# A recurrence beside a large product: sums written into PSUM ahead of the product, GpSimd's work moved, empty instructions spread

## The chip, the core and the metric

The kernel runs on one core of a Trainium2 chip. Five engines work side by side, each through its own list of instructions in order: TensorE (PE, with its weight loads shown as PEld), VectorE (DVE), ScalarE (ACT), GpSimd (POOL) and SyncE (SP), which here only starts DMA transfers. They wait for one another through semaphores. SBUF is the core's working memory, PSUM the memory that TensorE writes to, eight banks of 512 floats in each of 128 partitions. The metric is the time of the whole program on the device, in microseconds.

## The reference

All tensors are float32. With x of 64 x 256 x 1024 and a condition of 64 x 1024:

```python
xW = jnp.einsum('ntd,dh->nth', x, Wx) + b
def step(prev_h, xw):
    next_h = jnp.tanh(prev_h @ Wh + xw)      # 256 steps, one after the other
    return (next_h, next_h)
x = x + h_t                                   # layer 0: residual
# layer 1: a gate from the condition, on a Haar transform and its inverse
h = silu(cond @ W1.T + b1); gate = sigmoid(h @ W2.T + b2)
x = x + (v + a)    # a: v transformed, times gate, transformed back
```

The gate is the same for all coefficients of a channel, so the transform and its inverse cancel and the second layer is a factor (2 + gate) for each sequence and channel. What remains is a large product x @ Wx, a recurrence of 256 steps that each need h @ Wh, tanh and a residual, and a multiplication by the factor.

## The kernel before, in words

**Stages.** The first 12 steps (`ALONE`) and a stretch of plain products for the first 16 pairs of steps (`FIRST`) are set up code. The steady part runs from step 12 to 255 and takes about nine tenths of the time. Two steps make a pair; `xT[i]` is the input of pair i.

**The steps of h.** Each step is one h @ Wh by a scheme of seven products on quadrants (Strassen-Winograd). In the order of TensorE they are: m1 into `m16`, product 4 into `accs[2]`, product 2 into `accs[0]`, m5 into bank `main0`, m6 into `m16`, m7 into bank `main1`, product 3 into `accs[1]`. Between them ScalarE copies m1 to `y` (L989) and m6 to `u` (L1024), VectorE forms the four quadrants of h (L1010, L1027, L1028, L1032, L1035, L1038), ScalarE applies tanh (L971), VectorE transposes each quadrant (L975) and forms the sums for the next step (L244 to L247). `put_part` (L639) writes the next step's x @ Wx into the banks that accumulate.

**The products beside h.** x @ Wx is computed for later pairs by the same scheme on a larger scale, in the order of `ORDER`: units of two pairs, four units to a chunk (`U`), so 28 products of a chunk, numbered 0 to 27 here, four for each of the seven forms. One product (`Product.multiply`, L824) is 12 matmuls of 128x512 in fp32r: the float32 operands are split in high and low parts, four matmuls go into a bank `mixed`, eight into a bank `main`. Two steps of h and then 3 or 4 products make a group (`M`, `counts`, `beside_x`); a chunk of products is spread over eight groups as 3, 4, 3, 4 and so on. Weights of a form are 3 MB, loaded from DRAM by `load_weights` two forms ahead.

**Around a product.** `Form` prepares an operand three products ahead: VectorE masks the high bits (L795), forms x2 (L800) and x1 (L807), ScalarE casts x0 (L809); the form of p = 5 starts with a sum (L781). Afterwards `take_mixed` copies the bank `mixed` with ScalarE (L859) and GpSimd adds to it (L860) either a bias row or the state `u` of the unit; `finish` adds the bank `main` with VectorE (L868) and, for four forms, stores the result. `reload` brings it back in the layout of h. Other GpSimd work is put off to the first of the two steps (`pool_later`): differences of the quarters of x for p = 5 and 6 (L770), `u` plus or minus `v` after p = 6 and 7 (L876), and, as its first item, the scaling of a finished pair by the factor (L520, two instructions). The last product's `finish`, with the first half of a form (L795, L800), comes in the first step behind the copy of m1; its second half (L807, L809) behind the copy of m6 (`slot`).

**Order.** All engines of the steady part run in the order in which the program is written; none is planned by a scheduler.

**Alignment.** TensorE's instructions are fetched in blocks of 256 (`BLOCK`). `addr_align(BLOCK, PLACE)` fills up with empty instructions until the next one has place 60 in its block. It stands before the last two matmul positions of a group of 3 or 4, so that block edges fall at the same places of each group.

Of the kernel before, what the change touches and what calls it, by code (L numbers as in the profile page):

```python
# [61 lines left out]
P = 128  # L62
# [7 lines left out]
KB = B // 2  # L70
# [15 lines left out]
FORMS = 3  # L86
ORDER = (1, 2, 5, 6, 3, 7, 4)
BLOCK = 256
PLACE = 60
# [3 lines left out]
def tile_cond_resid(  # L93
# [425 lines left out]
    def scale(x, s: int) -> None:  # L519
        nc.gpsimd.tensor_mul(of_step(x, s), of_step(x, s), blocks(factor))  # L520
# [248 lines left out]
    def pool_sub(out, a, b) -> None:  # L769
        nc.gpsimd.tensor_sub(out, a, b)  # L770

    class Form:


        def __init__(self, n: int):
            self.n = n
            self.c, self.p, self.v = ups[n]
            a = {q: quarters.get((self.c, self.v, q)) for q in PLACES}
            if self.p == 5:
                self.src = forms.tile([P, HALF], F32, tag="s1", bufs=1, name=f"s1_{n}")  # L780
                nc.vector.tensor_add(self.src, a[21], a[22])  # L781
                self.later(lambda: (pool_sub(a[21], a[11], a[21]), pool_sub(a[11], a[22], a[21])))
            else:
                self.src = a[{1: 11, 2: 12, 6: 11, 3: 12, 7: 21, 4: 22}[self.p]]
            if self.p == 6:
                self.later(lambda: (pool_sub(a[12], a[12], a[11]), load_quarter(self.c + 1, self.v, 11)))
            made[n] = self
# [26 lines left out]
    class Product:  # L814
# [9 lines left out]
        def multiply(self, aligned: bool) -> None:  # L824
            f, w = made.pop(self.n), weights[self.m]

            def one(out, x, j: int, start: bool, stop: bool) -> None:
                for k in range(KB):
                    if aligned and j == 0 and k == KB - 2:
                        nc.tensor.addr_align(BLOCK, PLACE)  # L830
                    nc.tensor.matmul(  # L831
                        out=out,
                        lhsT=x[:, k * P : (k + 1) * P],
                        rhs=w[j][:, cols(k)],
                        start=start and k == 0,
                        stop=stop and k == KB - 1,
                    )

            one(self.mixed, f.x2, 2, True, True)
            one(self.main, f.x1, 1, True, False)  # L840
            one(self.main, f.x0, 0, False, True)
# [7 lines left out]

        def take_mixed(self) -> None:  # L850

            p = self.p
            if p in (1, 5):
                t = self.new_state("u" if p == 1 else "v")
                add = b_row[:, cols(0 if p == 1 else 1)]
            else:
                t = halves_x.tile([P, HALF], F32, tag="o", bufs=3, name=f"o_{self.n}")
                add = self.state("u")
            nc.scalar.activation(t, self.mixed, AF.Copy, scale=-1.0)  # L859
            nc.gpsimd.tensor_add(t, t, add)  # L860
            self.t = t
# [30 lines left out]
    slot = []  # L892

    def form(n: int, late: bool = False) -> None:

        f = Form(n)
        f.first()
        if late:
            slot.append(f.second)
        else:  # L900
            f.second()

    def prepare(late: bool = False) -> None:

        if formed[0] < min(len(ups), done[0] + FORMS):
            form(formed[0], late)
            formed[0] += 1

    def beside_x(t: int, n: int) -> None:

        before = None
        for j in range(n):
            m = done[0]
            u = Product(m, (n - 1 - j) % 2 ^ 1)
            u.multiply(n > 2 and j == n - 1)
            done[0] += 1
            if j == 0:
                residual(t, hT)
            if before and (before.c, before.v) == (u.c, u.v):
                before.finish()  # L920
                before = None
            u.take_mixed()
            if j == 0:
                accs[:] = [put_part(t + 1, o) for o in range(3)]
            if before:
                before.finish()
            before = u
            if last_of_product(m):
                load_weights(u.m + 2)
            if j + 1 < n:  # L930
                prepare()
        if n == 0:
            residual(t, hT)
            accs[:] = [put_part(t + 1, o) for o in range(3)]
        else:
            slot.append(lambda: (before.finish(), prepare(True)))
# [16 lines left out]
    counts = []  # L953
    for c, n in enumerate(UNITS):
        counts += [7 * n * (g + 1) // sizes[c] - 7 * n * g // sizes[c] for g in range(sizes[c])]
    groups = [M] * len(counts) + [2 * M]
    first = ALONE
    for t in range(ALONE, T):
# [30 lines left out]
        nc.scalar.copy(y[:, 0], m16)  # L989
        if slot:  # L990
            slot.pop(0)()
        if s == 0 and i > ALONE // S and i - 1 in pairs and i < NP - 1:
            scale(pairs[i - 1], 0)
            scale(pairs[i - 1], 1)
        if s == 0:
            for f in pool_later:
                f()
            pool_later.clear()
            if i + 1 < NP:
# [22 lines left out]
        put_next(0)  # L1022
        strassen_product(m16, sides[6], 6)
        nc.scalar.copy(u, m16)  # L1024
        if slot:
            slot.pop(0)()
# [76 lines left out]
```

## Time and profile before

| | us |
|---|---|
| time, median of 2 runs (3645.45 and 3645.54) | 3645.49 |
| the profiled execution's own time | 3618.79 |
| its span | 3616.7 |
| TensorE busy | 3092.5 |
| VectorE busy | 2654.7 |
| GpSimd busy | 1387.4 |
| ScalarE busy | 1050.9 |
| mean granted TensorE clock, share of full speed | 0.955 |

The profile is of one execution. Busy time is the time in which an engine has an instruction under way; a busy TensorE is not one at its peak, because matmuls overlap. The table of waits names for each wait the engine and line that waited, what ended the wait, the total, the number of times and the longest. "issue" means that nothing the profile shows ended it. The timeline lists instructions in order of time, with the idle time before them in brackets. A window is a stretch of the span with the busy time of each engine, the granted clock, and the share of time that the DMA engines were busy.

### The profile page before, as it was taken

The page shows a single profiled execution, that of the slowest core. Times are in us where ns is not written, and L with a number is a line of the kernel's source. Part 1 is how long each engine was busy: PE and PEld are TensorE (multiplying, and loading weights), DVE is VectorE, ACT ScalarE, POOL GpSimd, SP SyncE. Part 2 cuts the span into 40 slices and gives each one's busy share as a digit, 9 for nine tenths or more (in the row PEclk, how much of TensorE's full clock was granted, in tenths as well). Part 3 has the DMA queues.
Part 4 walks back from the last instruction along what each step waited for, and adds up shares of the span by engine and source line. Part 5 has one row for each costly group of instructions (what it writes and reads, how often), then busy time and mean ns, then how long its engine had stood idle before and what let it go on. Part 6 is the DMA issues. An engine that isn't in the chain of part 4 may idle for free.

```text
span 3616.7 us, 149916 instructions
## 1 busy us (share of the span) xinstructions
PE 3092.5 (86%) x63190; PEld 2674.6 (74%) x63190; DVE 2654.7 (73%) x6017; ACT 1050.9 (29%) x3097; POOL 1387.4 (38%) x985
## 2 busy tenths in 40 slices
PE   9976888888989888888888889888898888888788
PEld 6865777777777777777777777777777777777677
DVE  7553777877868677786777868678686777877665
ACT  3111223323323233332233323232232233322222
POOL 2241343543435344353443434335243343534231
PEclk9988999999999999999999999999999999999899
DMA  7555556565565656565465564655556565655565
GB/s 272 180 183 212 173 194 220 180 226 179 205 213 186 215 188 216 184 215 208 158 222 200 190 230 165 222 176 200 201 185 217 185 211 177 214 200 190 180 223 185
DMA packets 273087, 721.45 MB, mean 199 GB/s; under 512 B 56240, under 2 KB 122544, under 8 KB 232112
## 3 DMA queue, kind: packets, MB, share of 16 engines
q1 hardware_dynamic: 272288, 711.34, 56.6%
q8 instruction: 515, 8.44, 0.9%
q14 instruction: 140, 1.15, 0.1%
q10 hardware_dynamic: 144, 0.52, 0.0%
HBM read 553.39 MB, written 158.33 MB: 197 GB/s over the span
## 4 chain that ended last, share of the span: by engine, by line
PE 60%; DVE 14%; issue 14%; DMA 5%; POOL 3%; ACT 2%; SPq 1%; DVEq 0%; POOLq 0%; ACTq 0%
PE acc L214 15%; PE main L831 14%; PE m_h L214 10%; PE main_h L214 10%; PE mixed L831 7%; DMA w<-form 3%; DVE x L807 2%; PE main L293 2%; DVE high L795 2%; DVE y L1027 2%; POOL o L860 1%; ACT h L971 1%; DVE hT L975 1%; DVE h L1032 1%; PE m L214 1%
## 5 line engine op out<-in xcount | busy, mean ns | idle before, releaser
L831 PE MATMUL main<-w,x 128*128 128x512 f32 x3136 | 813.1, 396 | 167.6 <-issue 161.9
L831 PEld LDWEIGHTS main<-w,x 128*128 128x128 f32 x3136 | 580.0, 188 | 336.2 <-issue 205.5
L860 POOL TENSOR_TENSOR o<-o,u 128x512 f32<-128x512 f32 x280 | 388.1, 1386 | 959.6 <-ACT o L859 934.0
L971 ACT ACTIVATE h<-h 128x128 f32<-128x128 f32 x976 | 275.5, 306 | 842.8 <-DVE h L1010 611.5
L831 PE MATMUL mixed<-w,x 128*128 128x512 f32 x1568 | 434.6, 399 | 0.7 <-issue 0.7
L214 PE MATMUL m_h<-wh,hT 128*32 128x128 f32 x7808 | 299.2, 299 | 134.4 <-DVE s L247 47.4
L809 ACT CAST x<-high 128x512 fp32r<-128x512 f32 x392 | 243.8, 622 | 540.5 <-DVE high L795 480.7
L214 PEld LDWEIGHTS m_h<-wh,hT 128*32 128x32 f32 x7808 | 229.7, 119 | 204.6 <-issue 128.6
L214 PE MATMUL main_h<-t,s 128*32 128x128 f32 x7808 | 281.7, 277 | 90.1 <-issue 89.5
L214 PE MATMUL acc<-t,hT 128*32 128x128 f32 x8160 | 309.1, 296 | 53.7 <-DVE hT L975 45.5
L831 PEld LDWEIGHTS mixed<-w,x 128*128 128x128 f32 x1568 | 285.2, 188 | 77.9 <-issue 23.9
L795 DVE TENSOR_SCALAR high<-a 128x512 int32<-128x512 int32 x336 | 334.1, 994 | 11.8 <-DMA a<-xT 11.7
L800 DVE SCALAR_TENSOR_TENSOR x<-high,a 128x512 fp32r<-128x512 f32 x336 | 319.7, 951 | 29.0 <-DVE high L795 1.8
L975 DVE STREAM_TRANSPOSE hT<-h 128x128 f32<-128x128 f32 x972 | 298.0, 307 | 52.5 <-ACT h L971 52.3
L520 POOL TENSOR_TENSOR x<-x,factor 128x512 f32<-128x512 f32 x242 | 328.7, 1380 | 10.6 <-DVE x L644 5.7
L214 PEld LDWEIGHTS m_h<-t,s 128*32 128x32 f32 x7808 | 227.4, 114 | 125.1 <-issue 101.6
L214 PEld LDWEIGHTS acc<-t,hT 128*32 128x32 f32 x8160 | 258.4, 121 | 69.9 <-DVE hT L975 57.4
L214 PE MATMUL m_h<-t,s 128*32 128x128 f32 x7808 | 274.5, 282 | 17.2 <-ACT y L989 12.7
L214 PE MATMUL acc<-wh,hT 128*32 128x128 f32 x8160 | 284.8, 280 | 2.5 <-issue 2.5
L214 PE MATMUL acc<-wh,s 128*32 128x128 f32 x8160 | 279.7, 276 | 3.8 <-issue 3.8
L860 POOL TENSOR_TENSOR u<-u,b_row 128x512 f32<-128x512 f32 x56 | 87.0, 1553 | 507.1 <-ACT u L859 505.6
L214 PE MATMUL main_h<-wh,s 128*32 128x128 f32 x7808 | 274.9, 281 | 5.9 <-issue 5.9
(118 smaller groups left out, 4622.1 us busy)
## 6 DMA issues: line engine op xcount, KB each, us to landing
w<-form SPq DMA_DIRECT2D x315, 1024.0 KB, 8.2
x<-xT SPq DMA_DIRECT2D x137, 512.0 KB, 4.2
yT<-x SPq DMA_DIRECT2D x122, 512.0 KB, 10.6
a<-xT SPq DMA_DIRECT2D x224, 256.0 KB, 3.5
xw<-sum_b SPq DMA_DIRECT2D x896, 64.0 KB, 3.3
sum_b<-o SPq DMA_DIRECT2D x168, 256.0 KB, 3.3
sum_b<-u SPq DMA_DIRECT2D x56, 256.0 KB, 3.8
form<-wx SPq DMA_DIRECT2D x36, 256.0 KB, 5.7
```

The source lines that it names most:

```text
L214: nc.tensor.matmul(out=out[q * R : (q + 1) * R], lhsT=a[:, k * R : (k + 1) * R], rhs=wh_s.sides[i][k][:, q], start=first and k == 0, stop= ...
L293: nc.tensor.matmul(out=acc[h], lhsT=v[:, k * P : (k + 1) * P], rhs=wx_s[k][which][:, h * HALF : (h + 1) * HALF], start=start and k == 0, s ...
L520: nc.gpsimd.tensor_mul(of_step(x, s), of_step(x, s), blocks(factor))
L795: nc.vector.tensor_scalar(out=self.high, in0=self.src[:].bitcast(I32), scalar1=HIGH, scalar2=None, op0=ALU.bitwise_and)
L800: nc.vector.scalar_tensor_tensor(out=self.x2, in0=self.high, scalar=1.0 + DOWN, in1=self.src, op0=ALU.mult, op1=ALU.subtract)
L807: nc.vector.tensor_sub(self.x1, self.src, self.high)
L809: nc.scalar.copy(self.x0, self.high)
L831: nc.tensor.matmul(out=out, lhsT=x[:, k * P : (k + 1) * P], rhs=w[j][:, cols(k)], start=start and k == 0, stop=stop and k == KB - 1,)
L860: nc.gpsimd.tensor_add(t, t, add)
L971: nc.scalar.activation(quad(h, j), quad(h, j), AF.Tanh)
L975: nc.vector.transpose(quad(hT, j), quad(h, j))
L1027: nc.vector.tensor_add(y[:, 3], y[:, 3], u)
```

## The change

- A product's `mixed` bank no longer begins empty. `preload` has ScalarE write the negated bias row or state `u` into the bank before the product, whose first matmul no longer clears it; so the copy with scale -1 (`take_mixed`) yields the sum, and the GpSimd addition is gone. The first product of a group is written in the second step of h (`coming`), the others one product ahead.
- The list of GpSimd work in the first step is reordered, the differences and sums first and the scaling last, and its first instruction waits for ScalarE's copy of m1 (`behind`, `mark`).
- The last form of a group is prepared whole, and in the second step instead of in two halves in the first: `slot` is now emptied behind the copy of m1 alone, one entry a step.
- In `beside_x` the previous product's `finish` comes ahead of `take_mixed`, and the residual and `put_part` behind it.
- The alignment stands in every product of a group of 3 or 4, with places 39 (three) or 30 (four) apart that end at 70 (`SPREAD`, `PLACE`), and is given up after the first group of another size.
- `counts`: a group takes at least 3 products in full chunks, and rounding is upward: 4, 3, 4, 3 instead of 3, 4, 3, 4.

```diff
+SPREAD = {3: 15, 4: 6}
-PLACE = 60
+PLACE = 70
...
+    def behind(ins, other) -> None:
+        tc.add_manual_dep(
+            ins.ins,
+            other.ins.name,
+            mybir.DependencyInfo(mybir.DependencyClass.Sync, mybir.DependencyReason.DATA),
+            reason="GpSimd works beside the products of h",
+        )
...
-                    if aligned and j == 0 and k == KB - 2:
-                        nc.tensor.addr_align(BLOCK, PLACE)
+                    if place is not None and j == 0 and k == KB - 2:
+                        nc.tensor.addr_align(BLOCK, place % BLOCK)
...
-            one(self.mixed, f.x2, 2, True, True)
+            one(self.mixed, f.x2, 2, False, True)
...
+        def preload(self) -> None:
+            prior = {1: b_row[:, cols(0)], 5: b_row[:, cols(1)]}.get(self.p)
+            nc.scalar.activation(self.mixed, self.state("u") if prior is None else prior, AF.Copy, scale=-1.0)
+
         def take_mixed(self) -> None:
...
-            nc.scalar.activation(t, self.mixed, AF.Copy, scale=-1.0)
-            nc.gpsimd.tensor_add(t, t, add)
-            self.t = t
+            nc.scalar.activation(self.t, self.mixed, AF.Copy, scale=-1.0)
...
+    def coming(n: int) -> None:
+        if n:
+            products.append(Product(done[0], (n - 1) % 2 ^ 1))
+            products[0].preload()
+
     def beside_x(t: int, n: int) -> None:
         before = None
+        aligned[0] &= n in SPREAD
         for j in range(n):
             m = done[0]
-            u = Product(m, (n - 1 - j) % 2 ^ 1)
-            u.multiply(n > 2 and j == n - 1)
+            u = products.pop()
+            u.multiply(PLACE - (n - 1 - j) * (24 + SPREAD[n]) if aligned[0] else None)
             done[0] += 1
-            if j == 0:
-                residual(t, hT)
...
             if before:
                 before.finish()
             before = u
+            if j + 1 < n:
+                nxt = Product(m + 1, (n - 2 - j) % 2 ^ 1)
...
+                nxt.preload()
+                products.append(nxt)
+            if before:
+                u.take_mixed()
+            if j == 0:
+                residual(t, hT)
+                accs[:] = [put_part(t + 1, o) for o in range(3)]
...
-            slot.append(lambda: (before.finish(), prepare(True)))
+            slot.append(lambda: before.finish() if before else None)
+            slot.append(prepare)
...
-        counts += [7 * n * (g + 1) // sizes[c] - 7 * n * g // sizes[c] for g in range(sizes[c])]
+        for g in range(sizes[c]):
+            least = need + -(-7 * n * (g + 1) // sizes[c])
+            counts.append(min(len(ups), max(least, sum(counts) + 3 if n == U else 0)) - sum(counts))
+        need += 7 * n
...
-        nc.scalar.copy(y[:, 0], m16)
+        mark = nc.scalar.copy(y[:, 0], m16)
         if slot:
             slot.pop(0)()
-        if s == 0 and i > ALONE // S and i - 1 in pairs and i < NP - 1:
-            scale(pairs[i - 1], 0)
-            scale(pairs[i - 1], 1)
         if s == 0:
-            for f in pool_later:
-                f()
+            todo = list(pool_later)
             pool_later.clear()
+            if i > ALONE // S and i < NP - 1:
+                todo += [lambda r=r: scale(pairs[i - 1], r) for r in range(S)]
+            for k, do in enumerate(todo):
+                ins = do()
+                if k == 0:
+                    behind(ins, mark)
...
+        if last_of_group and not final:
+            coming(counts[0])
         strassen_product(m16, sides[6], 6)
         nc.scalar.copy(u, m16)
-        if slot:
-            slot.pop(0)()
```

## The prediction

> **What bounds the kernel now.** I read the page's head and chain first. TensorE (PE) is busy 86% of the span and holds 60% of the chain that ended last, but a seventh of that chain is "issue", time in which the engine waited for nothing that the profile names.
>
> ```profile
> span 3616.7 us, 149916 instructions
> PE 3092.5 (86%) x63190; PEld 2674.6 (74%) x63190; DVE 2654.7 (73%) x6017; ACT 1050.9 (29%) x3097; POOL 1387.4 (38%) x985
> PE 60%; DVE 14%; issue 14%; DMA 5%; POOL 3%; ACT 2%; SPq 1%; DVEq 0%; POOLq 0%; ACTq 0%
> ```
>
> GpSimd (POOL) is at 38%: its additions are off the chain, and taking them away gives nothing by itself. So I asked who PE waits for.
>
> ```profile
> PE main L831 <- issue: 161.9, 106, 7.6
> PE main_h L214 <- issue: 95.3, 48, 3.3
> PE m_h L214 <- DVE s L247: 47.4, 21, 2.5
> PE acc L214 <- DVE hT L975: 45.5, 41, 2.0
> ```
>
> The first row is the dearest wait, and it is the alignment's own. The trace holds runs of empty instructions on PE's sequencer, 110 runs beside x, 73.5 ns for each instruction: 50 to 52 (3.8 us) in a group of three products, 26 to 28 (1.9 us) in a group of four. Just behind them the last two matmuls of the group come 2.1 us late (three) or 0.35 us (four); PE's queue covers the first 1.65 us. A group's numbers close: 896 slots of two steps, 72 of three products, 4 to 6 waits and 50 to 52 empty ones make 1024.
>
> Then one period of eight groups by the table of windows, each from one start of products to the next (columns: time, busy us and instructions by engine, granted clock, DMA share, GB/s).
>
> ```profile
> 1943.56:1966.56 23.00, 21.02 (x488) 18.77 (x485) 17.65 (x47) 7.83 (x25) 6.82 (x5) 1.00 0.20 67
> 1966.56:1994.08 27.52, 24.13 (x501) 20.88 (x497) 24.67 (x53) 8.73 (x27) 14.57 (x10) 1.00 0.54 202
> 2044.97:2072.52 27.55, 23.13 (x489) 19.83 (x485) 18.27 (x47) 7.84 (x25) 9.96 (x7) 0.94 0.71 243
> 2072.52:2102.60 30.08, 25.87 (x501) 22.35 (x497) 21.78 (x51) 8.90 (x27) 9.62 (x7) 0.95 0.64 225
> ```
>
> The first is undisturbed but for its empty instructions: 8.5 us of products, 2.1 of gap, 12.3 of two h steps. The others have the same steps in 14 to 19 us. The timeline gives two reasons. **DMA:** in the last window,
>
> ```profile
> 2081.93 1.46 SPq L760 DMA_DIRECT2D w<-form  x3
> 2094.57 1.08 PE L214 MATMUL main_h<-t,s 128*32 128x128 f32 x31
> 2098.14 0.27 PE L214 MATMUL main_h<-t,s 128*32 128x128 f32 x1 [2.49 <-issue]
> ```
>
> 3 MB of weights are issued 2.2 us before the steps, and the DMA engines are full until about 2096. The 16 KB block with PE's next 256 instructions is asked for 256 instructions ahead (3.5 us in h): here its packet began 3.9 us after the block ahead was entered, and PE went on 2.3 us after that. In the quiet first window the packets begin 0.1 to 0.9 us after, and nothing stalls. **GpSimd against VectorE (DVE):**
>
> ```profile
> 1959.13 0.29 DVE L1027 TENSOR_TENSOR y<-y,u 128x128 f32<-128x128 f32 x1
> 1982.60 6.16 POOL L770 TENSOR_TENSOR a<-a,a 128x512 f32<-128x512 f32 x4
> 1986.21 1.35 DVE L1027 TENSOR_TENSOR y<-y,u 128x128 f32<-128x128 f32 x1
> ```
>
> A VectorE instruction that reads SBUF alone waits until the GpSimd instruction under way ends (0.29 becomes 1.35 us); those that read PSUM, and the transposes, keep their times.
>
> **The change part by part.** Durations are of the profiled execution (3618.8 us, of which 3616.7 are the span); the median of the timed runs is 3645.5, 0.7% longer, so I take differences from the profile and set them on the median.
>
> A. *Empty instructions spread.* By the orders of both programs they stay 4,350 (4,779), but no run is longer than 22 (1.62 us, at the first product of three; then 13 to 15 for each product; at most 10 with four). All lie under the 1.65 us that the queue covers, and 2.7 us apart it fills again. So the first row goes: -162 us. If it doesn't fill, the cost is what it was (bounds -162 to 0). Four-product groups give 0.35 us each of this, the five gaps over 7 us (behind groups of two) about 37 in all.
>
> B. *Clock.* The trace grants half the clock in 76 stretches, most of 3.41 us; 26 stand behind these gaps, each up to 1.7 us: -44 at most, 0 at least if another gap takes their place. I take -35, since most have no other gap near. By the Trainium skill ("TensorE: Matmul & The Clock Gate", What's actually happening) the clock falls only after an idle window of about 3.4 us; by that rule gaps of 2 us cost no clock and B is nothing. The trace disagrees: the window from 2044.97 shows 0.94 with no PE gap above 2.5 us.
>
> C. *Sums through PSUM.* 392 GpSimd additions (1.39 us) go and 392 ScalarE (ACT) writes into a bank come; nearest rows 0.59 us (PSUM to SBUF) and 0.58 (SBUF to PSUM, 128x512, L256), so 0.6. ScalarE then has 1.8 us of work for each product of 2.7: hidden. Its place: a group's first write stands in step two behind tanh of quadrant 0 and ahead of the copy of u; the next product's stands ahead of taking the present bank, ready over 1 us before its product. If ScalarE waited here, the copy of u and three tanh would. On its inputs it doesn't: u's GpSimd sum, where there is one, comes first in the list and ends by 2.9 us. Products lose waits on the main bank (rows of 4 to 12 us): counted at 0, bounds -12 and +13 (0.3 us in the third of groups whose step two ends late).
>
> D. *The last form moves from step one to step two.* In step one VectorE no longer runs L795 and L800 ahead of L1010, nor L807 ahead of L1027. In the second window (DVE late, no DMA stall) steps take 15.9 us instead of 12.3; I get 14.2 there, below. Thirteen such groups: -30 with what the others save (bounds -45, 0). In step two it costs 0.43+0.69+0.68 = 1.8 us between the residual (ends 2.7 us into the step) and L1010, which PE allows at 2.9: L1010 starts at 4.6, tanh and the first bank write end at 5.9, and products can start at 6.2. Hidden by 0.3 us, unless GpSimd is still at work.
>
> E. *GpSimd begun behind y's copy, sums of forms first, scales last.* It starts 1.5 us into step one, one instruction each 1.28 us when alone, and by turns with VectorE's SBUF instructions. Its list is 2 to 5 instructions long in six groups of eight (over by 8.2 us), 9 and 7 in two (forms 9 to 12; forms 13 to 15 with two sums of u). With 9: the turns put L1027 at 5.4 us, L244 to L247 at 8.2, 9.7, 11.2 and 12.7 (undisturbed 7.3 to 8.0), the residual at 14.2, the form at 14.9, L1010 at 16.7, tanh, bank write, and the products start at 18.0: 5.7 us over 12.3, before 1.8. With 7: 15.6, 3.3 over, before 1.5. Four, with a form that adds L781: products at 13.3 and up to 0.9 later in their bank waits. The two long lists cost 3.9+1.8 = 5.7 us a period, 13 periods: +74. Bounds 0 (a form's wait is hidden) and +110 (half clock behind the 4 us gap as well).
>
> F. *Groups are 4,3,4,3 instead of 3,4,3,4.* A weight load follows products 3, 7, 11 and so on of each 28. Before, the group of products 0 to 2 has none (23.00 us); now 0 to 3 ends with one, its DMA lying wholly over the two steps, as before only with product 27 (last window of the period, 29.23 us: steps 17.4). So +5 in that group; group 4 to 6 becomes free, but was without DMA stall already. The four others near h stay within 1 us of what they were: earlier by product, but without 2 us of gap as a head start. 13 periods at 5, less 5: +60 (bounds 0 and +90). The Trainium skill ("Runtime: NRT & Kernel Launch", Instruction fetch mechanics) has instruction fetch hidden by the slow issue; by it F is nothing. The 2.49 us row above speaks against it.
>
> PLACE 60 to 70 moves block edges by 10 slots, 0.14 us in h: nothing. The tail after the first group of two has no alignment; its edges fall anywhere, 11 groups, 0 +-10.
>
> Sum: -162-35-30+74+60 = -93. 3645.5-93 = **3552**.
>
> **Rivals.**
> 1. *The gain is kept*: E and F stay near 0, since the six short lists end before L244 and the loads find other gaps. For it: the second window's four subtractions cost before only through the form in step one, which is gone. Against it: the turns in the timeline. -162-35-30 = -227: 3418; half of it 3485.
> 2. *The change doesn't do what it says*: the queue doesn't fill between runs and the row of 161.9 stays. Against it, groups of four with 1.9 us of empty instructions lose only 0.35. Then -30+74+60: 3750; with E and F nothing, 3615.
> 3. *Slower*: the first product waits for the bank write, this for tanh, L1010 and a form that takes turns with GpSimd, in all groups and not in two of eight. It decides once GpSimd's work reaches 8 us into h everywhere, for instance with scales that wait. At the 3.3 us of the list of seven in 75 further groups: +248, 3800. Slower by over 2% from 2.2 us a group on. Against it: six lists end by 8.2 us.
> 4. *Clock by the skill's rule*: the gaps of 2 us cost no clock, so B is 0: 3587.
>
> **How the numbers follow.** Forecast 0.58 (3480 to 3640), rival 1 0.22, rival 2 0.08, rival 3 0.06, rival 4 0.06. A change of 2%, 73 us, is about what can be told from none here. Of the forecast six in ten lie below 3572.6: 0.35, with rival 1 0.57 faster. Slower by over 2%: half of rival 2 and all of 3, 0.10. The rest, 0.33, within. The range 3420 to 3670 leaves out the low end of rival 1 and the dear ends of 2 and 3.
>
> **What would show it.** A: the wait of the products' main bank on issue falls from 161.9 to below 30. B: 50 to 60 half-clock stretches for 76. C: no GpSimd line among the products, ScalarE's writes at 0.6 us. D: steps without long list or load near 12.3. E: one window in eight with steps near 18 and GpSimd busy over 12 us. F: the window of products 0 to 3 above 27 us with a stall on issue at main_h. The prediction is wrong if the products' first matmul waits for ScalarE in most groups, or if no steps take long beside a load.

## The result, and the profile after

The changed kernel took **3468.5 us** (median of 2 runs, 3466.1 and 3470.9), beside 3645.5 for the kernel before: a ratio of **0.9514, 95% interval 0.9474 to 0.9555**. The forecast was 3552 us with a range of 3420 to 3670, so the sign and the range held, but the gain is 177 us where the forecast had 93. It lies between rival 1 (3418) and its half (3485). The runs below show that the terms of the sum were wrong by more than their sum.

The page of the profiled execution (3466.1 us, mean granted clock 0.966 for 0.955), its head and its chain:

```profile
span 3464.3 us, 148882 instructions
...
PE 3061.6 (88%) x63190; PEld 2678.8 (77%) x63190; DVE 2348.7 (68%) x6017; ACT 1269.8 (37%) x3489; POOL 792.0 (23%) x593
...
q8 instruction: 513, 8.40, 1.0%
...
PE 74%; issue 10%; DVE 6%; DMA 5%; POOL 2%; ACT 2%; SPq 1%; DVEq 0%; POOLq 0%; ACTq 0%
```

PE now holds 74% of the chain (60%), VectorE 6% (14%). GpSimd lost 595 us of busy time, far more than the span lost. The waits of PE (columns: total us, times, longest):

```profile
PE main_h L215 <- issue: 142.2, 83, 3.6
PE acc L215 <- issue: 134.4, 81, 3.7
PE mixed L840 <- ACT mixed L863: 56.9, 30, 3.8
...
PE m_h L215 <- DVE s L247: 1.3, 2, 1.0
```

The row of 161.9 us of the products' main bank on issue is gone altogether. The rows of step one on VectorE (47.4, 45.5, 32.8) are gone or near 1 us. In their place stand two rows on issue within the steps, 277 us, and one of the first bank write.

The trace says what this issue is. The queue q8 on the page carries TensorE's instructions: its 513 packets of 16 KB are as many as TensorE's 131,447 instructions have blocks of 256. Each of the 164 stalls of the two rows ends 1.1 to 1.7 us after a packet of this queue has ended; of moments picked at random 9 in 100 lie so. They are waits for a block that comes late. (In the sums below a packet that ended over 1 us before the stall began does not count.) The same test takes apart the rows of before, because a wait is named after whatever the profile saw last: all 21 stalls on L247 (47.4 us) and 15 of the 25 on L246 (29.8 of 32.8 us) end so, and none of the 41 on L975. So most of the two rows under L247 and L246 was not VectorE. Counted by this test, late blocks take 222 us of the steps before and 283 after, and not the 110 and 277 of the rows on issue.

I cut each execution into three parts: what lies ahead of the first group, the products (all groups), and the steps of h between them. The last 4.6 us, behind TensorE's last matmul, are in no column.

| profiled execution, us | ahead | products | steps | span |
|---|---|---|---|---|
| before | 365.6 | 1302.2 | 1944.3 | 3616.7 |
| changed | 347.9 | 1134.6 | 1977.2 | 3464.3 |

The products fell by 167.6 us and the steps rose by 32.9. The part ahead was not changed by the edit; in the profiles of the experiments it ends anywhere from 348 to 366 us, so the 17.7 us there are variation.

One period by the table of windows, the four groups of products 0 to 3, 4 to 6, 7 to 10 and 11 to 13 (length, then busy us and instructions of PE, PEld, DVE, ACT and POOL, clock, DMA share, GB/s):

```profile
1444.09:1471.63 27.54, 24.15 (x499) 21.24 (x496) 17.83 (x50) 11.09 (x30) 2.53 (x2) 1.00 0.50 174
1471.63:1494.85 23.22, 21.44 (x488) 19.00 (x485) 17.33 (x49) 9.37 (x28) 5.10 (x4) 1.00 0.31 105
1494.85:1522.36 27.51, 23.89 (x499) 21.22 (x496) 22.84 (x47) 10.34 (x29) 11.99 (x9) 0.99 0.50 172
1522.36:1546.49 24.13, 23.00 (x485) 20.09 (x485) 17.94 (x46) 9.32 (x28) 8.84 (x7) 0.94 0.76 255
```

The first has a load beside its steps and is 4.5 us longer than the window that stood there before (23.00, with one product less). In the timeline of its steps, which begin at 1455.19:

```profile
1453.48 2.13 SPq L761 DMA_DIRECT2D w<-form  x3
...
1462.91 0.31 PE L215 MATMUL acc<-wh,s 128*32 128x128 f32 x3 [1.41 <-issue]
...
1468.66 0.38 PE L215 MATMUL main_h<-t,s 128*32 128x128 f32 x4 [1.98 <-issue]
```

The steps take 16.4 us where the first window of before had 12.3, and two stalls of 1.4 and 2.0 us are most of that, as part F had it. The third window has the list of nine (1505.96 is the start of its steps):

```profile
1507.44 9.27 POOL L771 TENSOR_TENSOR a<-a,a 128x512 f32<-128x512 f32 x7 [20.75 <-ACT y L1008]
...
1514.20 1.37 DVE L247 TENSOR_TENSOR s<-s,hT 128x128 f32<-128x128 f32 x1
...
1515.61 1.25 DVE L248 TENSOR_TENSOR s<-hT,s 128x128 f32<-128x128 f32 x1
...
1516.78 1.77 DVE L645 TENSOR_TENSOR x<-x,hT 128x512 f32<-128x512 f32 x1
...
1518.47 1.48 DVE L804 TENSOR_SCALAR high<-a 128x512 int32<-128x512 int32 x1
...
1521.19 0.28 DVE L1031 TENSOR_TENSOR h<-acc,y 128x128 f32<-128x128 f32 x1
...
1521.73 0.58 ACT L863 ACTIVATE mixed<-b_row 128x512 f32<-128x512 f32 x1
...
1522.36 2.08 PE L840 MATMUL mixed<-w,x 128*128 128x512 f32 x4 [3.62 <-ACT mixed L863]
```

This is part E step for step, 16.4 us to the products where 18.0 were worked out: VectorE's last sums by turns with GpSimd, the residual, the form, the first quadrant, the bank write, and PE waiting 3.6 us for it. So the terms D, E and F could be read off here as right in kind. The experiments show that two of them were still charged to the wrong part, and that the price of F is not made of late blocks.

### The profile page after: what moved, and what is told of

Its sections match the earlier page's. It is cut to its first block, busy times and chain, and to the rows that moved or that the text cites. A ratio compares the mean times of both kernels' runs of the same rounds, so it can differ in the third digit from the quotient of the medians.

```text
span 3464.3 us, 148882 instructions
## 1 busy us (share of the span) xinstructions
PE 3061.6 (88%) x63190; PEld 2678.8 (77%) x63190; DVE 2348.7 (68%) x6017; ACT 1269.8 (37%) x3489; POOL 792.0 (23%) x593
## 4 chain that ended last, share of the span: by engine, by line
PE 74%; issue 10%; DVE 6%; DMA 5%; POOL 2%; ACT 2%; SPq 1%; DVEq 0%; POOLq 0%; ACTq 0%
PE main L840 20%; PE acc L215 17%; PE m_h L215 12%; PE main_h L215 11%; PE mixed L840 10%; PE main L294 2%; PE m L215 1%; POOL a L771 1%; DVE x L816 1%; DMA a<-xT 1%; DVE x L645 1%; PE mixed L294 1%; DVE high L804 1%; SPq L898 1%; DMA xw<-sum_b 1%
## 5 line engine op out<-in xcount | busy, mean ns | idle before, releaser
L840 PE MATMUL main<-w,x 128*128 128x512 f32 x3136 | 791.6, 395 | 4.2 <-DVE y L1056 2.5
L840 PE MATMUL mixed<-w,x 128*128 128x512 f32 x1568 | 444.9, 406 | 57.3 <-ACT mixed L863 56.9
L215 PE MATMUL acc<-wh,s 128*32 128x128 f32 x8160 | 334.3, 282 | 125.6 <-issue 124.8
L771 POOL TENSOR_TENSOR a<-a,a 128x512 f32<-128x512 f32 x168 | 217.4, 1311 | 739.3 <-ACT y L1008 610.2
L215 PEld LDWEIGHTS acc<-wh,s 128*32 128x32 f32 x8160 | 269.0, 114 | 149.6 <-issue 148.9
L886 POOL TENSOR_TENSOR u<-u,v 128x512 f32<-128x512 f32 x112 | 146.7, 1324 | 997.0 <-ACT y L1008 372.4
L215 PEld LDWEIGHTS main_h<-t,s 128*32 128x32 f32 x7808 | 233.6, 110 | 164.9 <-issue 162.9
L215 PE MATMUL main_h<-wh,s 128*32 128x128 f32 x7808 | 299.2, 289 | 3.7 <-issue 3.7
L215 PE MATMUL m_h<-wh,hT 128*32 128x128 f32 x7808 | 281.4, 279 | 3.0 <-issue 3.0
L215 PEld LDWEIGHTS main_h<-wh,s 128*32 128x32 f32 x7808 | 255.7, 117 | 5.1 <-issue 4.7
L809 DVE SCALAR_TENSOR_TENSOR x<-high,a 128x512 fp32r<-128x512 f32 x336 | 238.5, 710 | 27.7 <-PE mixed L840 0.2
```

The source lines that it names most:

```text
L215: nc.tensor.matmul(out=out[q * R : (q + 1) * R], lhsT=a[:, k * R : (k + 1) * R], rhs=wh_s.sides[i][k][:, q], start=first and k == 0, stop= ...
L771: return nc.gpsimd.tensor_sub(out, a, b)
L809: nc.vector.scalar_tensor_tensor(out=self.x2, in0=self.high, scalar=1.0 + DOWN, in1=self.src, op0=ALU.mult, op1=ALU.subtract)
L840: nc.tensor.matmul(out=out, lhsT=x[:, k * P : (k + 1) * P], rhs=w[j][:, cols(k)], start=start and k == 0, stop=stop and k == KB - 1, skip_ ...
L886: when_h(self.c, lambda: (nc.gpsimd.tensor_add if p == 6 else nc.gpsimd.tensor_sub)(u, u, v))
```

## The experiments

The later chips ran the kernel before in 3634 to 3636 us, so I compare ratios to it and turn a difference of ratios into us with 3635; between two kernels it is good to 17 to 22 us, most of that from the changed kernel's own two runs. Sums over a trace are of one execution of each kernel. Letters are those of the prediction. Each part was undone in the changed kernel, two were done alone, and one run took the loads away.

**A alone** (in the kernel before):

```diff
+SPREAD = {3: 15, 4: 6}
...
-                    if aligned and j == 0 and k == KB - 2:
-                        nc.tensor.addr_align(BLOCK, PLACE)
+                    if place is not None and j == 0 and k == KB - 2:
+                        nc.tensor.addr_align(BLOCK, place % BLOCK)
...
-            u.multiply(n > 2 and j == n - 1)
+            u.multiply(PLACE - (n - 1 - j) * (24 + SPREAD[n]) if n > 2 else None)
```

> The kernel before with one edit, the empty instructions of a group of three or four spread over its products (part A alone; the gaps of some 7 us behind groups of two stay). My theory: the row of 161.9 us goes except for those five gaps (37 us), so -125, and half-clock stretches behind the gaps go with it, -35: 3645 - 160 = 3485 us (range 3450 to 3520), and the products' part of a period falls by about 9 us while the steps of h stay as they were. Rival: the gain of A needs the other parts (GpSimd's additions gone from the products), because products without gaps run into the wait for the main bank: 3560 to 3600 us, with a row of waits on the main bank in place of the row on issue.

Measured: 3539.1 us, ratio 0.9745 (0.9719 to 0.9772): 93 us less, and neither expectation. The products do what A says, 1138.1 us for 1302.2, 164 less, and the row on issue falls to the five gaps behind groups of two. But the steps rise from 1944.3 to 2019.8 us. **Nearly half of what the gaps cost comes back in the steps.** Most of it, 54 of 75 us, is late blocks, by the test above: 276 us of the steps for 222. They grow by 1.7 us behind products 10 to 13, 0.9 behind 14 to 16 and 1.3 behind 21 to 23. A smaller part is the other engines' work, which can be seen in a group of products 3 to 6. Before, with its steps beginning at 1541.00:

```profile
1540.61 0.59 ACT L859 ACTIVATE o<-mixed 128x512 f32<-128x512 f32 x1
...
1541.28 1.28 POOL L860 TENSOR_TENSOR o<-o,u 128x512 f32<-128x512 f32 x1 [2.36 <-ACT o L859]
...
1542.51 2.99 POOL L520 TENSOR_TENSOR x<-x,factor 128x512 f32<-128x512 f32 x2
1542.59 0.69 DVE L868 SCALAR_TENSOR_TENSOR o<-main,o 128x512 f32<-128x512 f32 x1 [0.60 <-POOL o L860]
...
1547.39 0.28 DVE L1010 TENSOR_TENSOR h<-acc,y 128x128 f32<-128x128 f32 x1
```

The last product's copy, its addition on GpSimd, its `finish`, then the half form and only then the first quadrant of h, L1010, 6.39 us into the steps. In the run with A alone, whose steps begin at 1502.82:

```profile
1502.91 0.59 ACT L860 ACTIVATE o<-mixed 128x512 f32<-128x512 f32 x1
...
1503.58 1.28 POOL L861 TENSOR_TENSOR o<-o,u 128x512 f32<-128x512 f32 x1 [2.36 <-ACT o L860]
...
1504.89 0.69 DVE L869 SCALAR_TENSOR_TENSOR o<-main,o 128x512 f32<-128x512 f32 x1 [0.60 <-POOL o L861]
...
1509.70 0.28 DVE L1011 TENSOR_TENSOR h<-acc,y 128x128 f32<-128x128 f32 x1
```

The chain is the same, and without the gap ahead of the last two matmuls the steps begin 0.5 us earlier against it: L1011 at 6.88 us. These steps are 2.0 us longer in all, and a stretch at half clock of 3.4 us, worth up to 1.7, begins 10.9 us into them. In groups of three, whose gap was 2.1 us, more of it moves: GpSimd's list after products 7 to 9 ends 12.1 us into the steps for 9.5, and these take 15.35 us for 14.19. Half-clock stretches fall only from 76 to 70, because others come in the steps, though 24 of the 26 behind the gaps are gone.

**A undone:**

```diff
-            u.multiply(PLACE - (n - 1 - j) * (24 + SPREAD[n]) if aligned[0] else None)
+            u.multiply(PLACE if aligned[0] and j == n - 1 else None)
```

> The changed kernel with the empty instructions back in one run ahead of the last two matmuls of a group (A undone, all else as changed). My theory: 3469 + 165 = 3634 us (3600 to 3650): nearly all of the change's gain is A with its clock, and the other parts come to about nothing together. Rival: the gain lies in the form's new place and the sums through PSUM as much as in A: 3530 to 3570 us.

Measured: 3515.3 us, 0.9674 (0.9645 to 0.9703), 58 us above the changed kernel. It lies beyond the rival's band: **the other parts together bring 119 us where the prediction had D, E and F cost 104.** The gap itself is smaller here. In groups of three, the sequencer stands 11.4 matmuls ahead of PE when the empty instructions begin, where it stood 6.5 ahead before, and the two matmuls around the gap start 1.31 us apart for 2.42. So the cover is not a fixed 1.65 us. I take it to depend on how early the last semaphore ahead of the gap was given, which no run takes alone.

**PLACE alone, and PLACE undone** (70 in the kernel before; 60 in the changed one):

```diff
-PLACE = 60
+PLACE = 70
```

The block edges of the two programs fall at different matmuls, which could explain the smaller gap and the row of 134 us on issue.

> The kernel before with PLACE 70 alone. Theory of the edge's place: in a group of three the edge moves from matmul 30 to 25, so TensorE's queue has five more matmuls (1.1 us) to fill again between the block's edge and the run of 50 to 52 empty instructions, and the gap falls from 2.1 to 1.0 us as in the run with the spread undone: 44 to 56 groups at 1.1 us, half of it given back in the steps, 3635 - 40 = 3595 us (3575 to 3615), main on issue falling from 162 to about 100. Rival, as the prediction had it: nothing, 3625 to 3645.

> The changed kernel with PLACE back at 60, so that block edges in the two steps fall at matmuls 48, 112 and 176 instead of 46, 110 and 174 (of 224; step two begins with 113). Theory of the edge's place: at 112 the wait for the block lies beside step two's own wait for hT, as before the change, where the acc row on issue held 14 us for 134 now; 20 to 60 us less, 3410 to 3450. Rival, as the prediction had it: 10 slots are nothing, and the time stays within 12 us of 3469 (the stalls only change their row).

Measured: 3620.9 us, 0.9957 (0.9927 to 0.9986) for 70 alone, with runs from 3594 to 3637; the row on issue stays at 161.9 us, so the smaller gap of the run above is not from the edge's place. And 3458.0 us, 0.9526 (0.9502 to 0.9550), for 60 in the changed kernel, the same as it. There the stalls only change their row: acc on issue falls from 134 to 14 us, and 110 us on VectorE's sums (L246 to L248) take its place. By the test above 50 of the 61 stalls in those three rows are late blocks all the same. The prediction's "nothing" holds in the changed kernel; 70 alone is 16 us faster, 0.4%.

**C undone:**

```diff
-            one(self.mixed, f.x2, 2, False, True)
+            one(self.mixed, f.x2, 2, True, True)
...
-            nc.scalar.activation(self.mixed, self.state("u") if prior is None else prior, AF.Copy, scale=-1.0)
...
             nc.scalar.activation(self.t, self.mixed, AF.Copy, scale=-1.0)
+            prior = {1: b_row[:, cols(0)], 5: b_row[:, cols(1)]}.get(self.p)
+            nc.gpsimd.tensor_add(self.t, self.t, self.state("u") if prior is None else prior)
```

> The changed kernel with the sums of other products again as GpSimd additions behind the copy of the bank mixed (C undone; bank mixed begins empty and ScalarE's write ahead of it is gone). By the prediction C is 0 (-12 to +13): 3455 to 3480 us. The theory after the first runs: the additions, 1.4 us each, put GpSimd's work beside the steps off by some 2 us and take turns with VectorE's last sums, so that C is worth 40 to 70 us: 3510 to 3540, with steps behind products 3, 10 and 21 1 to 2 us longer, as in the run with the spread alone.

Measured: 3523.7 us, 0.9702 (0.9676 to 0.9728): **C is worth 68 us**, where the prediction had 0 with bounds of -12 and +13. The size is the one expected, the place only in part. The steps behind products 18 to 27 are 0.7 to 1.4 us longer, but those behind 4 to 13 are shorter, since without a bank write the first matmul does not wait; it is the products that grow, 1218.4 us for 1134.6, most of all 7 to 10 (13.5 us for 11.4) and 11 to 13 (13.8 for 10.2). There PE starts and then stands still one bank later:

```profile
1536.43 1.20 PE L840 MATMUL mixed<-w,x 128*128 128x512 f32 x4
...
1541.06 3.75 PE L840 MATMUL main<-w,x 128*128 128x512 f32 x8 [3.43 <-DVE h L1054]
...
1547.23 1.44 POOL L872 TENSOR_TENSOR o<-o,u 128x512 f32<-128x512 f32 x1 [3.45 <-ACT o L870]
...
1551.70 0.69 DVE L879 SCALAR_TENSOR_TENSOR u<-main,o 128x512 f32<-128x512 f32 x1 [1.27 <-POOL o L872]
```

The eight matmuls behind that wait take 3.75 us for 1.98, and `finish` again waits for the addition. PE's waits for a main bank, 3.6 us in the changed kernel, are now rows such as this:

```profile
PE main L840 <- DVE h L1054: 38.7, 14, 3.5
```

Half-clock stretches are 67 for 59, and late blocks as before, 284 us for 283.

**D undone:**

```diff
+    def begin() -> None:
+        if formed[0] < min(len(ups), done[0] + FORMS):
+            f = Form(formed[0])
+            f.first()
+            slot.append(f.second)
+            formed[0] += 1
...
-            slot.append(lambda: before.finish() if before else None)
-            slot.append(prepare)
+            slot.append(lambda: (before.finish() if before else None, begin()))
...
         nc.scalar.copy(u, m16)
+        if slot:
+            slot.pop(0)()
```

> The changed kernel with the last form again in two halves in step one, behind the copies of m1 and u (D undone). By the prediction's D +30: 3500 us; the group of products 4 to 6 goes from 14.0 to about 16.5 us. Rival: since step two then has no form between a long GpSimd list and the first bank write, the groups that now wait 3.8 us (products 7 to 10) give back what the others lose: 3455 to 3480 us.

Measured: 3412.8 us, 0.9402 (0.9381 to 0.9423): **41 us faster than the changed kernel. D costs time, it does not save any**, and even the rival expected less of its going. Products 4 to 6 keep their steps (14.2 us for 14.0); behind 7 to 10 they fall from 16.4 to 14.4, and the wait of the first bank write falls from 56.9 to 4.2 us. With a list of eight, and steps that begin at 1474.68:

```profile
1484.78 1.34 DVE L247 TENSOR_TENSOR s<-s,hT 128x128 f32<-128x128 f32 x1
...
1486.16 1.25 DVE L248 TENSOR_TENSOR s<-hT,s 128x128 f32<-128x128 f32 x1
...
1487.33 0.68 DVE L645 TENSOR_TENSOR x<-x,hT 128x512 f32<-128x512 f32 x1
...
1487.93 0.28 DVE L1038 TENSOR_TENSOR h<-acc,y 128x128 f32<-128x128 f32 x1
```

The turns are there as in the changed kernel, but the first quadrant follows the residual at once, at 13.25 us, where the form in between put it at 15.23.

**The form elsewhere in step two**, behind the copy of u (where the first bank write is already issued):

```diff
-        if slot:
+        if len(slot) == 2:
             slot.pop(0)()
...
         nc.scalar.copy(u, m16)
+        if s == 1 and slot:
+            slot.pop(0)()
```

> The changed kernel with one edit: in step two the last form (mask, x2, x1, x0) stands behind the copy of u and the quadrant 0's tanh and the first bank write, not ahead of them. My theory (E): the first bank write no longer waits for a form that takes turns with GpSimd, so the 3.8 us wait behind a list of nine goes and the groups with seven lose theirs; the steps' own sums (L1033, L1048, L1049 and L1056) get 1.8 us later instead. The wait of the row mixed on ScalarE (56.9 us) falls below 15, half-clock stretches go with it, the time falls by 30 to 60 us, to 3410 to 3440. Rival: step two's quadrants 3, 2 and 1 are the bound there, and 1.8 us more on VectorE ahead of them are paid in most groups: 100 groups at 0.5 to 1 us, 3500 to 3550 us, with the bank write early and the products waiting for VectorE at the main bank.

Measured: 3504.7 us, 0.9646 (0.9621 to 0.9671), 48 us slower than the changed kernel: the rival. The steps behind 7 to 10 gain as expected (13.7 us for 16.4), and the products then wait for VectorE's quadrants at the main bank; two rows of 20.9 and 18.7 us appear there, where 2.5 stood. Neither of the two places tried in step two, ahead of the bank write and behind it, is as good as the halves in step one.

**E undone:**

```diff
             pool_later.clear()
             if i > ALONE // S and i < NP - 1:
-                todo += [lambda r=r: scale(pairs[i - 1], r) for r in range(S)]
-            for k, do in enumerate(todo):
-                ins = do()
-                if k == 0:
-                    behind(ins, mark)
+                todo = [lambda r=r: scale(pairs[i - 1], r) for r in range(S)] + todo
+            for do in todo:
+                do()
```

> The changed kernel with GpSimd's list as before: begun at once, the two scalings first (E undone; the form stays in step two). By the prediction's E (+74): 3395 to 3410 us. The theory after the first runs: the dear thing is the form in step two behind a list of nine or seven, and the list is as long as it was; begun 1.5 us earlier it ends 1.5 us earlier in two groups of eight, 20 us, so 3440 to 3470 us, with the wait of mixed on ScalarE at 30 to 57 us.

Measured: 3559.3 us, 0.9786 (0.9741 to 0.9830), 99 us slower than the changed kernel. Neither expectation held, not even in sign. **In the changed kernel E saves some 100 us; the prediction charged it 74.** Most of the loss lies in one place: products 7 to 10 take 19.3 us for 11.4, and their steps give 2.9 of that back. Their timeline:

```profile
1516.51 1.67 POOL L521 TENSOR_TENSOR x<-x,factor 128x512 f32<-128x512 f32 x1 [6.70 <-DVE x L645]
...
1517.07 1.40 DVE L804 TENSOR_SCALAR high<-s 128x512 int32<-128x512 int32 x1
...
1518.14 11.29 POOL L771 TENSOR_TENSOR a<-a,a 128x512 f32<-128x512 f32 x7
...
1518.57 1.57 DVE L809 SCALAR_TENSOR_TENSOR x<-high,s 128x512 fp32r<-128x512 f32 x1
...
1520.07 1.77 DVE L816 TENSOR_TENSOR x<-s,high 128x512 fp32r<-128x512 f32 x1
...
1522.49 2.09 PE L840 MATMUL main<-w,x 128*128 128x512 f32 x8 [1.57 <-DVE o L878]
```

The list no longer begins in the steps. It runs right through the products, where VectorE makes a form for each: three instructions of 0.43, 0.69 and 0.69 us become 1.40, 1.57 and 1.77, and the last two of these four products take 6.5 us each where one takes 2.7. Before, GpSimd's own additions stood ahead of the list in its order and held it back until 1.5 us into the steps (the scaling began at 1542.51, right behind the addition of 1541.28). C takes these away, and E's wait puts the list back where it had been. By these timelines C and E belong together; both undone at once was not run.

**F undone:**

```diff
-            least = need + -(-7 * n * (g + 1) // sizes[c])
+            least = need + 7 * n * (g + 1) // sizes[c]
```

> The changed kernel with the numbers of products in a group rounded down again, 3, 4, 3, 4 (F undone). My theory: the group of products 0 to 3, whose steps took 16.3 us beside a weight load where products 0 to 2 had 12.6, gets its quiet steps back, 3.7 us in each of 13 periods: 3469 - 48 = 3421 us (3400 to 3445). Rival: the loads' stalls only move on to other groups (a group of 14 to 16 or 21 to 23 takes them), and the time stays within 10 us of 3469.

Measured: 3420.9 us, 0.9417 (0.9387 to 0.9447), as expected: **F costs 35 us**. The steps behind the first group of a period are 12.4 us again for 16.3, and those of the other groups hold, in sum. But the stalls do what the rival said. Late blocks come to 298 us for 283: the 3.3 us behind the first group go, 2.0 come behind products 7 to 9, where 7 to 10 had none, and 0.7 to 0.8 more each behind those of 10 to 13, 14 to 16 and 21 to 23. What falls is the wait of the first bank write, from 56.9 to 25.1 us, and the half-clock stretches, from 59 to 32 (234 to 147 us, worth up to 43). Which of the two carries the 35 us was not tested.

**The loads taken away** (products reuse the first two forms):

```diff
-        if m < 7 * len(UNITS):
+        if 2 <= m < 7 * len(UNITS):
+            weights[m] = weights[m - 2]
+        elif m < 2:
             weights[m] = {}
```

> The changed kernel without the loads of the weight forms after the first two (left out: 103 of 105 forms; the products reuse the two that are there, so this is a time without 300 MB of transfers and not the reference's output). Theory (F): the waits on issue in the steps (main_h 142 us, acc 134) are blocks of instructions that come late while the loads fill the DMA engines; both rows fall below 25 us, and the time by 200 to 270: 3200 to 3270 us, with steps near 12.3 us in groups 0 to 3 and 25 to 27. Rival: a block's edge costs this by itself, and the loads only move it: the rows stay above 100 us together and the time falls by less than 60.

Measured: 3185.7 us in one run, 0.876 of before on that chip, which is some 273 us below the changed kernel and a little beyond the theory's band. The waits of this run:

```profile
PE mixed L842 <- ACT mixed L865: 66.8, 34, 4.1
PE main_h L215 <- issue: 41.9, 53, 2.8
...
PE acc L215 <- issue: 21.0, 32, 3.0
```

The two rows on issue fall from 277 to 63 us; main_h stays above the 25 expected. The steps behind products 0 to 3 take 12.4 us, those behind 18 to 20 12.8 for 16.9. Late blocks in the steps fall from 283 to 49 us. That the stalls are waits for instruction blocks, and that most of them come with the loads, is shown. That the blocks wait behind the loads in the DMA engines is what the traces fit; the run takes the transfers away and with them all else that they delay, such as the scalings' inputs.

**D and F undone together**, and then GpSimd's list begun at once in its new order:

```diff
-            for k, do in enumerate(todo):
-                ins = do()
-                if k == 0:
-                    behind(ins, mark)
+            for do in todo:
+                do()
```

> The changed kernel with two parts undone: the form in two halves in step one (D undone) and the products 3, 4, 3, 4 (F undone). If the two parts cost in different groups (D behind products 7 to 10, F behind 0 to 3), their gains of 41 and 35 to 48 us add: 3360 to 3385 us. Rival: both gains are the same slack (the loads' place against the steps), 3405 to 3425.

> As the run with the halves and 3, 4, 3, 4, and GpSimd's list, in the changed order, begun at once and not behind the copy of m1. If the start counts: long lists end 1.5 us earlier and the turns with VectorE's last sums are fewer, 10 to 25 us less than that run. Rival: VectorE's forms of the products' last finish at the start of step one then take turns with GpSimd, and nothing is won: within 8 us of it.

Measured: 3386.2 us, 0.9311 (0.9286 to 0.9337) for the first, the fastest kernel of the study: 74 us below the changed one, where the two gains alone add up to 76. Against the runs with one of them undone, D is worth 39 us here and F 33, and these two differences do without the changed kernel's runs. The products take 1110.7 us and the steps 1911.9, less than before the change. In its group of products 3 to 6, steps from 1457.28:

```profile
1457.45 0.69 DVE L878 SCALAR_TENSOR_TENSOR o<-main,o 128x512 f32<-128x512 f32 x1 [0.86 <-PE main L840]
...
1458.06 0.68 DVE L790 TENSOR_TENSOR s<-a,a 128x512 f32<-128x512 f32 x1
...
1461.95 0.28 DVE L1038 TENSOR_TENSOR h<-acc,y 128x128 f32<-128x128 f32 x1
```

`finish` waits for PE alone and begins 0.17 us into the steps instead of 1.59 before; the first quadrant comes at 4.67 us for 6.39, with the form's half still ahead of it. And 3463.9 us, 0.9526 (0.9499 to 0.9553) for the second: 78 us are lost by the wait's absence alone, against both expectations, again mostly at one place, behind products 7 to 9 (steps of 18.4 us for 14.7, products of 9.8 for 8.4).

## Why the prediction was right in sign and wrong in its terms

| part | predicted, us | price in the changed kernel, by undoing it |
|---|---|---|
| A and its clock B | -197 | -58 (alone in the kernel before: -93) |
| C | 0 (-12 to +13) | -68 |
| D | -30 (-45 to 0) | +41 |
| E | +74 (0 to +110) | -99 |
| F | +60 (0 to +90) | +35 |
| PLACE | 0 | 0 within 17 (alone in the kernel before: -16) |

The prices do not add up, because A, C and E lean on one another: the kernel with these three (and PLACE and the new order in `beside_x`) is 250 us faster than before, and D and F then give 74 back. The prediction had -123 for the three and +30 for the two, and reached a sum half as large with signs of D and E that the runs reverse. The sign of the forecast rests on A alone, which does save time, but less than C or E. That the range held is in part luck: A was overrated by 139 us and D by 71, C and E together were underrated by 241.

- **A, right about the row, wrong about its worth.** The step that failed is "so the first row goes: -162 us". The row went, and the products fell by 168. But a wait on the path is worth its length only if nothing stands behind it. Alone, A gave back 75 us in the steps, and in the changed kernel 40 (1937.1 us with A undone, 1977.2 with it). Of the 75, 54 are late instruction blocks, which had been fewer behind the gaps; of the 40 it is 32 (252 to 283 us), though two executions can differ by that much, since PLACE 60, with an equal time, has 252 as well. Why a gap ahead of the steps keeps the blocks in time was not tested. The rest is work that ran beside the gap, the last product's copy, addition and `finish`, for which the first quadrant of h waits. A row that said this part was in the trace of before: the wait of L868 on L860, 1.6 us into the steps.
- **Cover of 1.65 us.** It was read as a size of PE's queue. It is how far the sequencer was ahead at the time, 6.5 matmuls before and 11.4 with the other parts. For the spread runs it made no difference.
- **B, right in size.** Half-clock stretches fell from 76 to 59 (50 to 60 expected), 328 to 234 us; at half speed that is up to 47 us, for 35. That it came so near is luck: A alone leaves 70 (328 to 296 us, up to 16), since others come in the steps, and the rest went with the other parts. The rule of the Trainium skill ("TensorE: Matmul & The Clock Gate", What's actually happening), by which the clock falls only after an idle window of about 3.4 us, is not what the traces show: 27 of the 59 have a stall on issue at main_h as the longest gap in the 5 us ahead of them, and most of these are 2.0 to 2.9 us long.
- **C, wrong.** I looked for it in the products' bank waits and in ScalarE's time, both near nothing, as forecast. The step that failed is "counted at 0": the addition stood between the last product and the first quadrant of the next step, and it kept VectorE's `finish` from freeing banks. What I worked out as D's gain, 14.2 us for 15.9 in the second window, comes without D: that window has 14.3 us in the run with D and F undone, and 18.3 with A alone, so it comes with C and E, or with the new order in `beside_x` that came with them. The two timelines show how; C by itself was not taken away there.
- **D, wrong in sign.** "Hidden by 0.3 us, unless GpSimd is still at work" was the right condition. The price of its failing was put under E.
- **E, right in its mechanism, charged to the wrong part.** The turns and the bank write behind the list of nine came as worked out, in 16.4 us for 18.0, and these groups cost 4.7 us a period where 5.7 were forecast (2.2 in the steps behind 7 to 10, 1.8 in the next products, at half clock in part, 0.7 behind them). But the list begins no later than it did before; what makes it dear is the form behind it, D. What E does by itself I did not ask: which instruction held the list back before, and what will once C removes it.
- **F, right about its group, wrong about the sum.** The group of products 0 to 3 has 3.3 us of late blocks that go when F is undone. But the four others near h do not "stay within 1 us of what they were": with 3, 4, 3, 4 other groups take the stalls, and the sum is 298 us for 283. The 61 us by which late blocks rose with the change are near the +60 of the prediction, but A alone brings 54 of them, and undoing F takes none away. F's own 35 us lie in the first bank write's wait, in the clock, or in both. The Trainium skill ("Runtime: NRT & Kernel Launch", Instruction fetch mechanics) has the fetch hidden by the slow issue, by which F would be nothing; the rows on issue, 277 us with the loads and 63 without, speak against it here.
- Of the signs listed in the prediction all came, or nearly (steps of 16.4 us beside the long list for 18), but one: 12.3 us in steps without a long list or load. Those behind products 4 to 6 take 14.0, of which 1.0 is late blocks.

## What to carry to other kernels

Before a gap is priced at its length, look for what else ended in it and who waits for that, instruction blocks included: here nearly half of 162 us came back. A wait is named after what was seen last, so test the name before building on it: here 77 us of late instruction blocks stood under VectorE's sums. When an instruction is removed from an engine that runs in order, ask what was queued behind it and will now start earlier, and beside what; the additions off the chain had kept the long list out of the products. Prices found by undoing one part are valid beside the other parts only, so try the parts that compete for one place (here the form in step two, and the group beside a load) separately before keeping them.

## What the hardware showed that I had not expected

- PE's sequencer ran 6.5 matmuls ahead in one program and 11.4 in another at the same place, and the same 50 to 52 empty instructions (73.5 ns each) cost 2.42 or 1.31 us from start to start. The likely reason, that banks are freed earlier without the additions, was not run by itself.
- GpSimd beside VectorE costs VectorE more than it costs itself: a form of 1.8 us took 4.7 while GpSimd's own seven instructions took 1.6 us each for 1.3.
- Taking 324 MB of loads off a core whose hardware DMA queue took 59% of the engines' span saved some 273 us; 214 of these show as stalls of PE on issue.
- PE goes on 1.1 to 1.7 us after the packet with its next instructions has ended, in all 164 stalls on issue in the changed kernel's steps and in all 85 without the loads. The profile can name such a stall after another engine.
- Behind PE gaps of 1.9 us and more the clock is halved at times: in the kernel before and in the changed one no half-clock stretch has only shorter gaps in the 5 us ahead of it, save one of each with none. Taking gaps away at one place brings them at another: 76, 70, 59, 45, 37, 32 in before, A alone, changed, D undone, D and F undone, F undone.
